# New places for tail rows, the second piece of T1 and tiles of x, and another last tile in a four-layer graph network

## The chip, the cores and the metric

The kernel runs on one core of one Trainium2 chip. The metric is the device time of one execution in microseconds (us), where a smaller number is better. Three timed runs of the kernel before gave 2122.76, 2124.17 and 2127.33 us, so the median is 2124.17 us.

The core has a matrix engine (TensorE, "PE" in the profile, with its weight loads shown as "PEld"), three engines for other arithmetic (VectorE "DVE", ScalarE "ACT", GpSimd "POOL") and SyncE "SP". Each works through its own list of instructions in order and waits on semaphores. SP and POOL also issue the transfers between the memory outside the core (DRAM) and the core's buffer (SBUF). The sums of matrix products arrive in PSUM, of which this kernel uses five banks under the tag `agg`, two under `out` and one under `sm`.

## The reference

There are N = 2708 nodes with 512 features. Each of four layers normalizes x by row, applies relu, multiplies by the adjacency matrix and by a weight, and adds the result to x:

```python
h = relu(layernorm(x)); x = x + relu((dinv[:, None] * (adj + I) * dinv[None, :]) @ h @ W0)
h = relu(layernorm(x)); x = x + (dis[:, None] * adj * dis[None, :]) @ h @ W1.T + b1
h = relu(layernorm(x)); x = x + relu((dinv[:, None] * (adj + I) * dinv[None, :]) @ h @ W2)
h = relu(layernorm(x))
# layer 3: attention over the edges (x_a) and a plain aggregation (x_b), each with a gate
x = x + sigmoid(attn_a * (softmax_like(scores, adj != 0) @ (h @ W_sa)) + attn_b * (adj @ (h @ W_g) + b_g))
```

Here `dinv` and `dis` are reciprocal roots of the row sums of adj, with 1 and with 1e-8 added.

## The kernel before, in words

**Tiling.** The 2708 rows are cut into four quarters of 677. A quarter holds five full tiles of 128 rows (`KT = 5`, 20 full tiles in all) and 37 tail rows. The tails of all quarters share two more tiles: tile `NF = 20` has 32 rows from each quarter, and tile `NF + 1` has the last 5 rows of each, padded to 8. The columns of a quarter are handled in two pieces of `W = 339`, numbered u = 0 and 1. A block of the transposed adjacency matrix is a 128 x 5 x 339 array in fp32, 848 KB.

**The aggregation** computes the transpose of adj @ h into `agg`. The 20 full tiles go through a product scheme with 7 in place of 8 multiplications, on two levels. The outer level forms sums of blocks named y11, y21, y22, t1, t2, t3 and t4. For each of these and each u, `inner_x` and `inner_y` form the sums of the inner level (DVE, lines 447 to 485), and `multiply` (line 515) runs seven products of ten matmuls each into banks pa, pb, pc and pd. `give` hands the results on to `agg`. `inner_y` takes four blocks o11, o12, o21 and o22. It writes t1, t2 and t4 to a pool of three buffers and t3 to a place that it is given, or into o12 where it is given none.

**The first aggregation** (`first_aggregate`, line 662) also builds the t sums and stores them in DRAM (`keep_o`, line 418, on POOL's queue), because later layers load them. Its last part is what the change touches:

1. u = 0 of the product with t4 is made. The four blocks of t2 become those of t1 by taking away y22, one block at a time (`third_less`, the subtraction at line 828). The blocks of y22 pass through two buffers, `y22[0]` and `y22[1]`.
2. `tails(True, (0, 1), rows)` adds the products of the tail rows for quarters 0 and 1 (lines 571 and 576, `agg` additions at line 621). `tail_rows` loads the rows of a quarter and adds a piece of the identity to them (line 600, DVE). Those of quarter 0 are loaded early. Those of quarter 1 go to a block from `free`, which at that point is `y22[0]`. They are two transfers of 339 KB, in runs of 2712 bytes.
3. The four blocks of T1 for u = 1 are loaded (`accumulated`: a load by SP, then a transfer by POOL that adds another block, line 712). Their places are `t4[3]`, `more[2]`, `y22[1]` and `y22[0]`.
4. Product 5 (with T1) runs for u = 0 and 1. For u = 0 its t3 goes to the place `own_t3`. A sum over half of h, `XC += XA` (line 868), stands between the two.
5. `tails(True, (2, 3), rows)` follows, then the epilogue of the first half of the tiles, product 3 with XC, and the epilogue of the rest.

**The epilogues** of layers 0 to 2 (`next_x`, line 893) go through tiles in groups of three. `load_x` brings a tile of x to one of four places of 512 columns (`xt_places`, taken in turn, POOL's queue, line 890). PE multiplies by the weight (line 883), ACT applies relu and the scale (line 903) into one of two places `y`, DVE adds it to x (line 908) and takes statistics, POOL stores x (line 909), and after the group ACT writes the normalized tiles to h (line 223). All these places, like `misc` (four times 512 columns) and `bg_bc` (512 columns, for a bias of layer 3), are slices of one tile `ends`. `misc` holds the bias of layer 1 in its first quarter and, from layer 2 on, four vectors of scores (`score_vectors`). The two vectors for quarters 2 and 3 of `misc` are loaded at line 968, and the bias at line 1044.

**Layer 3's last stage** (line 1163) runs 40 steps over the quarters, and each tile of the output is finished by `attention` (line 1111): load x and the gated sum, one short matmul for the row sum, a projection by `W_sa` (512 columns, 8 matmul instructions), three operations on DVE and ACT, and the store. Five tiles are left after the last step: 17, 18 and 19, then tail tiles 20 and 21. A tail tile first collects its columns with copies on DVE (`tile_cols`, lines 174 and 160) into the two places `y`, and leaves through four stores, one for each quarter.

**Order.** A scheduler fixes the order of each engine's instructions when the program is compiled. It takes what it holds to be ready first, with earlier lines first among the ready. `tc.issue_after(ins)` puts the instructions of a block behind `ins` on the same engine's list.

Of the kernel before, what the change touches and what calls it, by code (L numbers as in the profile page):

```python
# [8 lines left out]
FP = mybir.dt.float32  # L9
AF = mybir.ActivationFunctionType  # L10
ALU = mybir.AluOpType

P = 128
D = 512
NC = D // P
# [6 lines left out]
U = 2  # L22
W = (Q + 1) // U
NF = NQ * KT
# [13 lines left out]
def gnn_kernel(  # L38
# [20 lines left out]
    nc = tc.nc  # L59
# [10 lines left out]
    ps_out = ctx.enter_context(tc.tile_pool(name="ps_out", bufs=2, space=bass.MemoryType.PSUM))  # L70
# [40 lines left out]
    agg = big.tile([P, 2, 2, 2, 2, U * W], FP, name="agg")  # L111
# [12 lines left out]
    free = list(in_obuf)  # L124
    more = [block(ends, k * BLK) for k in range(3)]
    own_t3 = block(ends, 3 * BLK)
# [5 lines left out]
    misc, ends_o = ends[:, ends_o : ends_o + 4 * D], ends_o + 4 * D  # L132
    xt_places = [ends[:, ends_o + k * D : ends_o + (k + 1) * D] for k in range(GT + 1)]
# [3 lines left out]
    bg_bc = ends[:, ends_o : ends_o + D]  # L137
# [10 lines left out]
    def load_w(w):  # L148
        w_sb = w_place[:, 0 : NC * D].rearrange("p (c o) -> p c o", c=NC)
        nc.gpsimd.dma_start(w_sb, w.rearrange("(c p) o -> p c o", p=P))  # L150
        return w_sb

    def full_cols(a, t):
        k = t % KT
        return a[:, k * P : (k + 1) * P]
# [7 lines left out]
    def tile_cols(a, t):  # L163

        cs = [a[:, f, :, c] for f in range(a.shape[1]) for c in range(a.shape[3])]
        if t < NF:
            q = t // KT
            return [full_cols(c[:, q // 2, q % 2], t) for c in cs]
        o, m = (KT * P, R0) if t == NF else (KT * P + R0 - PAD, R1P)
        if a.shape[5] == R0 + R1:  # L170
            o -= KT * P
        g = new_y().rearrange("p (c n) -> p c n", c=NC)
        for c, src in enumerate(cs):
            nc.vector.tensor_copy(
                g[:, c, 0 : NQ * m].rearrange("p (i q r) -> p i q r", i=2, q=2),
                src[:, :, :, o : o + m],
            )
        repeat(g[:, 0 : len(cs)], NQ * m)
        return [g[:, c] for c in range(len(cs))]
# [133 lines left out]
    y11 = {}  # L313
# [78 lines left out]
    XA = h[:, 0:half, 0 : D // 2]  # L392
    XB = h[:, 0:half, D // 2 : D]
    XC = h[:, half:NF, 0 : D // 2]
# [12 lines left out]
    QUAD = [(0, 0), (0, 1), (1, 0), (1, 1)]  # L407
# [36 lines left out]
    at_v, at_u2, at_u3, at_end, at_shift, at_y, at_pe = [], [], [], [], [], [], []  # L444
# [26 lines left out]
    def inner_y(blks, u, loops, t3=None, t3_first=False):  # L471
        o11, o12, o21, o22 = blks
        if loops:
            add_loops(o11, u, loops)
            add_loops(o22, u, loops)
        t1, t2, t4 = (tpool.tile([P, KT, W], FP, tag="t", name=f"t{k}") for k in (1, 2, 4))
        t3 = o12 if t3 is None else t3
        if t3_first:
            nc.vector.tensor_add(t3, o22, o12)
        nc.vector.tensor_add(t1, o12, o11)  # L480
        nc.vector.tensor_add(t2, o22, t1)  # L481
        at_y.append(nc.vector.tensor_add(t4, o21, t2).ins)  # L482
        if not t3_first:
            at_y[-1] = nc.vector.tensor_add(t3, o22, o12).ins
        return {1: o11, 2: o21, 3: o22, 4: t4, 5: t1, 6: t2, 7: t3}
# [94 lines left out]
    def tail_rows(self_loops, q, pieces=None):  # L580


        blk = None
        if pieces is None:
            blk = free.pop(0)
            both = blk[:, 0 : 2 * U].rearrange("p (s u) w -> p s u w", s=2)
            pieces = [both[:, :, u] for u in range(U)]
            for s in range(2):
                nc.sync.dma_start(both[:, s], yt[s, :, q])
        else:  # L590
            for u in range(U):
                load_tails(q, u, pieces[u])
        if self_loops:
            o = (KT * P) % W
            for s, i, c0, n in (
                (0, ident[:, q * R0 : (q + 1) * R0], o, R0),
                (1, again_ident[:, q * R1P + PAD : (q + 1) * R1P], o + R0, R1),
            ):
                d = pieces[U - 1][:, s, c0 : c0 + n]
                nc.vector.tensor_add(d, d, i)  # L600
        return blk, pieces
# [60 lines left out]
    def first_aggregate(epilogue):  # L662
# [9 lines left out]
        pieces = [(q, u) for q in range(2) for u in range(U)]  # L672
        t3 = {0: early[:2]}
        places = spare + early[2:]
        for q, u in pieces:
# [14 lines left out]
            if (q, u) == (1, 0):  # L690
                ys = inner_y([y11[a, b, u] for a, b in QUAD], u, 0, own_t3, True)
# [12 lines left out]
        def accumulated(blks, key, u, source):  # L704

            for (a, b), blk in blks.items():
                if key in PLAIN:
                    load_plain(key, a, b, u, blk)
                else:
                    nc.sync.dma_start(blk, osum[key, a, b, u])  # L710
                j, i = PLAIN[source]
                last = nc.gpsimd.dma_start(blk, yb[j + a, i + b, u], accum_op=ALU.add)
            return last.ins

        def keep_all(blks, key, u, a_b=QUAD):
            for a, b in a_b:
                keep_o(blks[QUAD.index((a, b))], key, a, b, u)
# [8 lines left out]
        came = {}  # L726
# [116 lines left out]
                    )  # L843
        for k, y in ((0, y22[0]), (1, y22[1]), (2, y22[0]), (3, y22[1])):
            minus_y22 = third_less(k, y, at_y[-1])
        free += y22
        with tc.issue_after(at_end[-1]):
            rows = [early_rows, tail_rows(True, 1)]
        tails(True, (0, 1), rows)
        t1 = [t2u, [t4[3], more[2], free.pop(0), free.pop(0)]]  # L850
        assert not free
        came = accumulated({QUAD[k]: t1[1][k] for k in (0, 1, 3, 2)}, "y12", 1, "y11")
        with tc.issue_after(at_end[-1]):
            nc.vector.tensor_add(agg[:, 1, 0], agg[:, 1, 0], agg[:, 1, 1])
        xs_ = inner_x(XB)
        p5 = [(0, 1, "less"), (1, 1, "less")]
        for u in range(U):
            more_loops = OUTER[5][2] - (OUTER[6][2] if u == 0 else 0)
            if u == 1:
                with tc.issue_after(came):  # L860
                    keep_all(t1[u], "t1", u, QUAD[1:3])
            with tc.issue_after(minus_y22 if u == 0 else at_end[-3]):
                ys = inner_y(t1[u], u, more_loops, own_t3 if u == 0 else None)
            keep_all(t1[u], "t1", u, QUAD if u == 0 else QUAD[::3])
            multiply(xs_, ys, u, p5)
            if u == 0:
                with tc.issue_after(at_end[-1]):
                    nc.vector.tensor_add(XC, XC, XA)
        free += t2u + [f for f in t1[1] if f is not more[2]]
        with tc.issue_after(at_end[-3]):  # L870
            rows = [tail_rows(True, q) for q in (2, 3)]
# [7 lines left out]
    def project(w_sb, t):  # L879
        cs = tile_cols(agg, t)  # L880
        po = ps_out.tile([P, D], FP, tag="out", name="po")
        for c in range(NC):
            nc.tensor.matmul(  # L883
                po, cs[c], w_sb[:, c, :], start=(c == 0), stop=(c == NC - 1)
            )
        return po, cs
# [32 lines left out]
                    after(t)  # L919


    w_sb = []

    def first_epilogue(ts):
# [60 lines left out]
    def keep_h(t):  # L985
        nc.gpsimd.dma_start(hs[t], h[:, t, :])
        h_dots(behind.get(t, ()))

    w2_sb = load_w(w2)
    vs = None  # L990

# [47 lines left out]
    def again(ts, fs):  # L1039

        for t in ts:
            nc.sync.dma_start(h[:, t, fs], hs[t][:, fs])

    nc.gpsimd.dma_start(bg_bc, bg.partition_broadcast(P))
    parts = {1: range(12, 14), 7: range(14, 17), 2: range(17, 20), 4: range(20, NT)}
    hooks = {p: lambda ts=ts: h_dots(ts) for p, ts in parts.items()}
# [55 lines left out]
    def place(t):  # L1102

        if t < NF:
            o = (t // KT) * Q + (t % KT) * P
            return [(0, P, o)]
        if t == NF:
            return [(q * R0, R0, q * Q + KT * P) for q in range(NQ)]
        return [(q * R1P + PAD, R1, q * Q + KT * P + R0) for q in range(NQ)]

    def attention(t, columns):
        xt = load_x(t, xs)
        y = load_x(t, xbs)
        nc.scalar.activation(xt, xt, AF.Copy, bias=0.5)
        sm = ps_sm.tile([P, NT], FP, tag="sm", name="pse")
        nc.tensor.matmul(sm[:, 0:1], columns(t), ones[:, 0:1], start=True, stop=True)
        pE, _ = project(wsa_sb, t)
        g = small.tile([P, 1], FP, tag="ge", name="ge")
        nc.vector.tensor_add(g, sm[:, 0:1], eps[:, t : t + 1])
        nc.vector.reciprocal(g, g)  # L1120
        nc.vector.tensor_mul(g, g, ga[:, t, 0:1])
        nc.vector.scalar_tensor_tensor(y, pE, g, y, ALU.mult, ALU.add)
        nc.scalar.activation(y, y, AF.Tanh, scale=0.5)
        nc.vector.scalar_tensor_tensor(xt, y, 0.5, xt, ALU.mult, ALU.add)
        for o, n, to in place(t):
            nc.gpsimd.dma_start(out[to : to + n, :], xt[o : o + n, :])

    sums = misc[:, 0 : 2 * U * W + NQ * (R0 + R1)]
    tail_sums = sums[:, 2 * U * W :].rearrange("p (f i c q r) -> p f i c q r", f=1, i=2, c=1, q=2)
# [32 lines left out]
    todo = []  # L1162
    for n, (q, u, b) in enumerate(steps):
# [35 lines left out]
        elif todo:  # L1199
            t, se_t = todo.pop(0)  # L1200
            attention(t, lambda t, se_t=se_t: full_cols(se_t, t))
    for t, se_t in todo:
        attention(t, lambda t, se_t=se_t: full_cols(se_t, t))
    for t in (NF, NF + 1):
        attention(t, lambda t: tile_cols(tail_sums, t)[0])


# [59 lines left out]
```

## Time and profile before

| What | Value |
|---|---|
| Timed runs, median | 2124.17 us |
| Profiled execution, its own time | 2125.74 us |
| Its span, first to last instruction | 2123.7 us |
| DVE busy | 1412.9 us |
| ACT busy | 406.0 us |
| POOL busy | 182.3 us |
| DMA, mean rate over the span | 170 GB/s |
| Mean granted clock of PE | 0.994 |

The profile describes one execution. Its span leaves out 2.0 us of the execution's own time, and the execution is 1.6 us above the median of the timed runs. A line of the timeline gives the start, the duration, the engine, the source line, the operation, what it writes and reads with the shapes, and in brackets the idle time of the engine just before it with what ended that idle time. A line of the waits gives the waiting instruction, what it waited for, the total in us, the number of times and the longest. "L600" is line 600 of the kernel.

### The profile page before, as it was taken

The page shows a single profiled execution, that of the slowest core. Times are in us where ns is not written, and L with a number is a line of the kernel's source. Part 1 is how long each engine was busy: PE and PEld are TensorE (multiplying, and loading weights), DVE is VectorE, ACT ScalarE, POOL GpSimd, SP SyncE. Part 2 cuts the span into 40 slices and gives each one's busy share as a digit, 9 for nine tenths or more (in the row PEclk, how much of TensorE's full clock was granted, in tenths as well). Part 3 has the DMA queues.
Part 4 walks back from the last instruction along what each step waited for, and adds up shares of the span by engine and source line. Part 5 has one row for each costly group of instructions (what it writes and reads, how often), then busy time and mean ns, then how long its engine had stood idle before and what let it go on. Part 6 is the DMA issues. An engine that isn't in the chain of part 4 may idle for free.

```text
span 2123.7 us, 20033 instructions
## 1 busy us (share of the span) xinstructions
PE 2064.4 (97%) x7320; PEld 1286.0 (61%) x7320; DVE 1412.9 (67%) x2486; ACT 406.0 (19%) x826; POOL 182.3 (9%) x329
## 2 busy tenths in 40 slices
PE   5999989999999999999999999999999999999998
PEld 2666645546666554666664556666777666666664
DVE  4578866656777767866685789867538755566512
ACT  1430001130000011100002120000117533444401
POOL 0110111120000011100002130000001000000001
PEclk9999999999999999999999999999999999999999
DMA  9998593545545444655444565545451223232212
GB/s 368 299 373 269 186 337 124 193 172 182 178 157 177 138 171 139 229 176 173 164 143 165 198 219 175 181 164 177 154 174 74 92 89 117 87 108 90 84 37 65
DMA packets 79442, 360.86 MB, mean 170 GB/s; under 512 B 10620, under 2 KB 15100, under 8 KB 79216
## 3 DMA queue, kind: packets, MB, share of 16 engines
q1 hardware_dynamic: 50384, 245.43, 33.8%
q0 software_dynamic: 28960, 114.15, 16.6%
q8 instruction: 58, 0.95, 0.2%
q14 instruction: 40, 0.33, 0.0%
HBM read 294.61 MB, written 62.15 MB: 168 GB/s over the span
## 4 chain that ended last, share of the span: by engine, by line
issue 45%; PE 39%; DMA 7%; DVE 5%; POOL 3%; ACT 0%; POOLq 0%; SPq 0%; DVEq 0%; ACTq 0%
PE pa L509 9%; PE pc L509 9%; PE pd L509 9%; PE pb L509 5%; PE po L883 3%; DMA obuf<-in_yb_dram 2%; PE pt L571 2%; DMA ends<-xs 2%; PE pg L1022 1%; DMA obuf<-in_yt_dram 1%; POOL ends L890 1%; POOL xs L909 1%; DVE ends L908 1%; PE pt L576 1%; DVE ends L975 1%
## 5 line engine op out<-in xcount | busy, mean ns | idle before, releaser
L1174 PE MATMUL pe<-obuf,h 128*128 128x339 f32 x1280 | 372.8, 448 | 0.0
L509 PE MATMUL pa<-obuf,h 128*128 128x339 f32 x1040 | 316.4, 448 | 2.9 <-ACT v L543 1.5
L1174 PEld LDWEIGHTS pe<-obuf,h 128*128 128x128 f32 x1280 | 240.9, 189 | 126.6 <-issue 10.0
L883 PE MATMUL po<-ends,agg 128*128 128x512 f32 x640 | 281.7, 596 | 4.6 <-ACT ends L903 4.3
L509 PEld LDWEIGHTS pa<-obuf,h 128*128 128x128 f32 x1040 | 196.1, 189 | 107.9 <-issue 6.9
L883 PEld LDWEIGHTS po<-ends,agg 128*128 128x128 f32 x640 | 119.6, 190 | 147.8 <-issue 137.5
L1095 ACT ACTIVATE e<-r,nsr 128x339 f32<-128x339 f32 x352 | 170.7, 566 | 27.4 <-DVE obuf L1099 11.6
L509 PE MATMUL pb<-t,s 128*128 128x339 f32 x560 | 171.1, 452 | 2.6 <-DVE t L481 2.6
L509 PE MATMUL pc<-t,h 128*128 128x339 f32 x560 | 169.4, 448 | 2.7 <-DVE u L556 2.7
L509 PE MATMUL pd<-t,s 128*128 128x339 f32 x560 | 169.2, 448 | 0.0
L509 PE MATMUL pd<-obuf,s 128*128 128x339 f32 x550 | 166.5, 448 | 1.9 <-DVE agg L530 1.9
L543 ACT COPY v<-pa 128x339 f32<-128x339 f32 x56 | 24.6, 440 | 733.7 <-PE pa L509 730.7
L509 PEld LDWEIGHTS pb<-t,s 128*128 128x128 f32 x560 | 106.3, 191 | 57.9 <-DVE t L481 4.0
L509 PEld LDWEIGHTS pc<-t,h 128*128 128x128 f32 x560 | 105.8, 189 | 57.7 <-DVE u L556 3.8
L509 PEld LDWEIGHTS pd<-t,s 128*128 128x128 f32 x560 | 105.9, 189 | 54.4 <-issue 0.5
L509 PEld LDWEIGHTS pd<-obuf,s 128*128 128x128 f32 x550 | 104.0, 189 | 55.8 <-DVE agg L530 3.4
L509 PE MATMUL pc<-obuf,s 128*128 128x339 f32 x440 | 133.1, 448 | 0.0
L509 PEld LDWEIGHTS pc<-obuf,s 128*128 128x128 f32 x440 | 83.3, 189 | 42.8 <-issue 0.5
L481 DVE TENSOR_TENSOR t<-obuf,t 128x1695 f32<-128x1695 f32 x55 | 105.4, 1916 | 0.0
L909 POOL DMA_DIRECT2D xs<-ends x66 | 35.9, 544 | 797.4 <-DVE ends L908 713.6
L482 DVE TENSOR_TENSOR t<-obuf,t 128x1695 f32<-128x1695 f32 x52 | 99.6, 1916 | 0.1
L1191 DVE COPY agg<-pe 128x339 f32<-128x339 f32 x16 | 7.5, 506 | 138.1 <-PE pe L576 138.1
(262 smaller groups left out, 2300.3 us busy)
## 6 DMA issues: line engine op xcount, KB each, us to landing
obuf<-in_yb_dram SPq DMA_DIRECT2D x132, 847.5 KB, 4.5
obuf<-osumt SPq DMA_DIRECT2D x100, 847.5 KB, 4.4
osumt<-obuf POOLq DMA_DIRECT2D x22, 847.5 KB, 11.0
xs<-ends POOLq DMA_DIRECT2D x66, 256.0 KB, 2.3
ends<-xs POOLq DMA_DIRECT2D x66, 256.0 KB, 3.5
obuf<-in_yt_dram SPq DMA_DIRECT2D x30, 339.0 KB, 3.6
obuf<-in_yb_dram POOLq DMA_DIRECT2D x11, 847.5 KB, 10.2
ends<-in_yb_dram SPq DMA_DIRECT2D x9, 847.5 KB, 9.2
```

Source lines behind the costliest of these rows:

```text
L481: nc.vector.tensor_add(t2, o22, t1)
L482: at_y.append(nc.vector.tensor_add(t4, o21, t2).ins)
L509: last = nc.tensor.matmul(ps, x[:, k, :], y[:, k, :], start=start and k == 0, stop=k == KT - 1, skip_group_check=not start,)
L543: at_v.append(nc.scalar.copy(v, pa).ins)
L571: nc.tensor.matmul(ps[c], h[:, NF, c * P : (c + 1) * P], tl[:, 0, :], start=start, stop=False)
L576: nc.tensor.matmul(ps[c], h[g, NF + 1, c * P : (c + 1) * P], tl[g, 1, :], start=False, stop=True)
L883: nc.tensor.matmul(po, cs[c], w_sb[:, c, :], start=(c == 0), stop=(c == NC - 1))
L890: nc.gpsimd.dma_start(xt, src[t])
L908: nc.vector.tensor_add(xt, xt, y)
L909: nc.gpsimd.dma_start(xs[t], xt)
L1095: nc.scalar.activation(e[:, k], row, AF.Exp, bias=nsr[:, t, s : s + 1], scale=1.0)
L1174: nc.tensor.matmul(pe[c], h[:, t, c * P : (c + 1) * P], a, start=(t == 0), stop=False)
```

## The change

It has four groups of edits.

- **Tail rows of quarter 1** go to the first four slices of `own_t3`, as two pieces with two transfers each (four of 173 KB, in runs of 1356 bytes). They, with the identity additions, are queued behind the last subtraction of y22 and no longer behind the last `give` of t4.
- **T1.** The blocks for u = 1 get the places `y22[0]`, `more[2]`, `y22[1]` and `t4[3]`, loaded in the order 1, 0, 2, 3. For u = 0, t3 is formed in o12 itself, and o12 and o21 are stored before `inner_y`. `XC += XA` moves behind the sums of u = 1.
- **Places for x.** Layers 0 and 1 get seven (quarters 2 and 3 of `misc`, and `bg_bc`, are added), layer 2 five (`bg_bc`), layer 3 four until its last step. The loads of lines 968 and 1044 then wait until those uses are over.
- **The end.** The five last tiles get twelve places in four blocks of `obuf`. The order becomes 17, 21, 18, 20, 19, and tile 19 is projected, finished and stored by halves of 256 columns.

```diff
-        free += y22
-        with tc.issue_after(at_end[-1]):
-            rows = [early_rows, tail_rows(True, 1)]
+        own = own_t3[:, 0 : 2 * U].rearrange("p (s u) w -> p s u w", s=2)
+        with tc.issue_after(minus_y22):
+            rows = [early_rows, tail_rows(True, 1, [own[:, :, u] for u in range(U)])]
         tails(True, (0, 1), rows)
-        t1 = [t2u, [t4[3], more[2], free.pop(0), free.pop(0)]]
+        t1 = [t2u, [y22[0], more[2], y22[1], t4[3]]]
         assert not free
-        came = accumulated({QUAD[k]: t1[1][k] for k in (0, 1, 3, 2)}, "y12", 1, "y11")
+        came = accumulated({QUAD[k]: t1[1][k] for k in (1, 0, 2, 3)}, "y12", 1, "y11")
...
-            if u == 1:
-                with tc.issue_after(came):
-                    keep_all(t1[u], "t1", u, QUAD[1:3])
+            with tc.issue_after(came) if u == 1 else nullcontext():
+                keep_all(t1[u], "t1", u, QUAD[1:3])
             with tc.issue_after(minus_y22 if u == 0 else at_end[-3]):
-                ys = inner_y(t1[u], u, more_loops, own_t3 if u == 0 else None)
-            keep_all(t1[u], "t1", u, QUAD if u == 0 else QUAD[::3])
+                ys = inner_y(t1[u], u, more_loops)
+            keep_all(t1[u], "t1", u, QUAD[::3])
             multiply(xs_, ys, u, p5)
-            if u == 0:
-                with tc.issue_after(at_end[-1]):
-                    nc.vector.tensor_add(XC, XC, XA)
+        with tc.issue_after(at_y[-1]):
+            nc.vector.tensor_add(XC, XC, XA)
...
+    misc_places = [misc[:, k * D : (k + 1) * D] for k in (2, 3)]
+    xt_places += misc_places + [bg_bc]
...
+    xt_places = [p for p in xt_places if not any(p is m for m in misc_places)]
     w2_sb = load_w(w2)
...
+    xt_places = [p for p in xt_places if p is not bg_bc]
     nc.gpsimd.dma_start(bg_bc, bg.partition_broadcast(P))
...
-    def attention(t, columns):
+    def attention(t, columns, pieces=1):
...
-        pE, _ = project(wsa_sb, t)
+        cs = tile_cols(agg, t)
...
-        nc.vector.scalar_tensor_tensor(y, pE, g, y, ALU.mult, ALU.add)
-        nc.scalar.activation(y, y, AF.Tanh, scale=0.5)
-        nc.vector.scalar_tensor_tensor(xt, y, 0.5, xt, ALU.mult, ALU.add)
-        for o, n, to in place(t):
-            nc.gpsimd.dma_start(out[to : to + n, :], xt[o : o + n, :])
+        n = D // pieces
+        for k in range(pieces):
+            f = slice(k * n, (k + 1) * n)
+            pE = ps_out.tile([P, n], FP, tag="out", name="pE")
+            for c in range(NC):
+                nc.tensor.matmul(pE, cs[c], wsa_sb[:, c, f], start=(c == 0), stop=(c == NC - 1))
+            nc.vector.scalar_tensor_tensor(y[:, f], pE, g, y[:, f], ALU.mult, ALU.add)
+            nc.scalar.activation(y[:, f], y[:, f], AF.Tanh, scale=0.5)
+            nc.vector.scalar_tensor_tensor(xt[:, f], y[:, f], 0.5, xt[:, f], ALU.mult, ALU.add)
+            for o, m, to in place(t):
+                nc.gpsimd.dma_start(out[to : to + m, f], xt[o : o + m, f])
...
-    for t, se_t in todo:
-        attention(t, lambda t, se_t=se_t: full_cols(se_t, t))
-    for t in (NF, NF + 1):
-        attention(t, lambda t: tile_cols(tail_sums, t)[0])
+    flat = [blk.rearrange("p k w -> p (k w)") for blk in free[:4]]
+    xt_places = [a[:, k * D : (k + 1) * D] for a in flat for k in range(3)]
+    todo = [(t, lambda t, se_t=se_t: full_cols(se_t, t)) for t, se_t in todo]
+    for k, t in ((1, NF + 1), (3, NF)):
+        todo.insert(k, (t, lambda t: tile_cols(tail_sums, t)[0]))
+    for n, (t, columns) in enumerate(todo):
+        attention(t, columns, 1 if n + 1 < len(todo) else 2)
```

## The prediction

> **What bounds the kernel now.** I read the page's busy times first, then everything PE waited for, then the timeline around the two places that the diff touches.
>
> ```profile
> PE 2064.4 (97%) x7320; PEld 1286.0 (61%) x7320; DVE 1412.9 (67%) x2486; ACT 406.0 (19%) x826; POOL 182.3 (9%) x329
> ```
>
> PE is the bound. No edit takes a matmul away, so a gain can only come from PE's idle time, from a slow clock after it, or from what follows PE's last matmul. PE's waits, longest first:
>
> ```profile
> PE pt L571 <- DVE agg L621: 7.4, 2, 6.6
> PE po L883 <- ACT ends L903: 4.3, 3, 2.0
> PE pc L509 <- DVE u L556: 2.7, 2, 2.0
> PE pb L509 <- DVE t L481: 2.6, 2, 2.2
> PE pd L509 <- DVE agg L530: 1.9, 1, 1.9
> PE pc L509 <- DVE ends L484: 1.8, 1, 1.8
> PE po L883 <- DVE ends L160: 1.8, 1, 1.8
> ```
>
> The 6.6 us wait is the largest after the start of the program. In the timeline, DVE's list shows its cause:
>
> ```profile
> 272.54 0.19 DVE L600 TENSOR_TENSOR obuf<-obuf,ident 128x32 f32<-128x32 f32 x1 [1.32 <-DMA obuf<-in_yt_dram]
> 275.54 0.17 DVE L600 TENSOR_TENSOR obuf<-obuf,again_ident 128x5 f32<-128x5 f32 x1 [2.80 <-DMA obuf<-in_yt_dram]
> ...
> 278.19 1.75 DVE L621 TENSOR_TENSOR agg<-agg,pt 128x339 f32<-128x339 f32 x4
> ...
> 278.74 2.63 PE L571 MATMUL pt<-tl,h 128*128 128x339 f32 x4 [6.63 <-DVE agg L621]
> ```
>
> L600 waits for quarter 1's tail rows; two sums (L468, L480) and then the L621 that frees PE's bank stand behind it. After the idle time PE also runs slowly (columns: time, PE busy, clock, DMA share, GB/s):
>
> ```profile
> 278.74:284.73 5.99, 5.99 (x16) 0.50 1.05 383
> ```
>
> Half a clock for 6.0 us costs 3.0 us of PE's work. DMA is full at the same time, its packets split evenly between POOL's queue q0 and SP's q1 from 264 to 276 us:
>
> ```profile
> q0 software_dynamic: 437, 2.60, 70.8%
> q1 hardware_dynamic: 408, 1.40, 31.8%
> ```
>
> The end, from the timeline:
>
> ```profile
> 2110.54 5.40 PE L883 MATMUL po<-ends 128*128 128x512 f32 x8 [1.82 <-DVE ends L160]
> ...
> 2115.97 0.75 DVE L1122 SCALAR_TENSOR_TENSOR ends<-po,ge,ends 128x512 f32<-128x512 f32 x1 [3.03 <-PE po L883]
> ...
> 2118.40 2.01 POOL L1126 DMA_DIRECT2D out_dram<-ends  x4 [3.17 <-DVE ends L1124]
> ```
>
> The last projection starts 1.82 us late and takes 5.40 us where the four before it take 3.68.
>
> **What the Trainium skill says.** "TensorE: Matmul & The Clock Gate", Part 1: a monitor with a free-running window of 3.4 us halves PE's clock after idling and restores it after a busy window. The trace agrees, at 284.73 and again at the end, where 1.82 us of idling was enough. The same page, on the engine queues: ACT and DVE are strictly first in, first out; the trace shows L468 held behind L600. "DMA: Bandwidth & Descriptors", Queues, rings and completion order: an engine takes descriptors of one ring in order and alternates between rings by packet; 437 against 408 packets agree.
>
> **The end.** Twelve places let the ten loads of the five tiles be issued while the last step runs, so no x or xbs load is late (before, L1114 waited 4.36, 2.83 and 2.87 us). Tail tiles 21 and 20 come second and fourth, so their copies (four of L174 at 0.17 to 0.26 us, two of L160 at 0.23 and 0.29) run beside a full tile's 3.66 us of PE; the place y they need is free one tile earlier. PE then runs five projections without a gap: 2093.93 + 5 x 3.66 = 2112.2 instead of 2115.95 (halves cost nothing: 257-column matmuls at L1022 ran at 25.53 / 117 = 0.218 us, half of 512 columns' 0.43). For the last half, DVE, ACT and DVE take an estimated 0.40, 0.37 and 0.36 us by size (from 0.75, 0.63, 0.69) and 0.4 of gaps: 1.5 instead of 2.45. One store issue takes 0.55 instead of 2.01; the four of tile 20 leave POOL at about 2113.1, before it. The 3.3 us after the last issue stay. End: 2112.2 + 1.5 + 0.55 + 3.3 = 2117.6, **-6.1 us**; bounds -7 and -3 (if one copy chain still stalls PE and slows the clock).
>
> **T1, second piece.** For u = 1 PE idles 0.53 (L543), 2.23 (L481) and 1.84 us (L484), 4.6 in all. The late block was the one in `y22[0]`: its load was issued at 290.44, after PE had read the tail rows there, and the added block landed at 312.18. Now it can be loaded from 263.94, when the third subtraction ends; even behind everything on SP's ring I put the last added block before 300, 10 us ahead of need. `XC += XA` (2.82 us) leaves the list before L482 and L484. DVE's list then has L480 and L481 ready 4.0 us after product 5's first piece ends and L484 at 8.6, where PE wants them at 4.1 and 9.3: only about 0.7 is left, **-3.9**; bounds -4.6 and 0. The moved sum lies behind L484 beside some 9 us of PE work. The in-place t3 waits for the store of o12, issued at 260.39 and landed at 274.19, before L484's 281.69; uncovered, each us late is paid. The two stores moved ahead are the ones that POOL issued first anyway.
>
> **Tail rows of quarter 1.** They can be issued from 258.7 (PE done with `own_t3`), 5 us earlier. But SP's ring already holds y22's last block until about 265, and POOL's ring holds an adding block (packets of 525 ns until 269.5) and the stores of T1. With runs of 1356 instead of 2712 bytes the rows are 512 packets instead of 256, and alternation gives them one for each of q0's. Estimate: 8 per DMA engine beside the adding block (8 x 0.585 = 4.7 us), 16 beside the two stores (16 x 0.305 = 4.9), 8 alone (0.5): 265 + 10.1 = 275.1, and with the lag of 1 to 2 us seen before about 276.5, against 275.5 now. The wait stays. L600 may also now stand before the loop additions L431 (six, 1.1 us) and the last give L530 (0.4), which then follow the wait. L621 comes 1 to 3 us later, PE's slow stretch overlaps more of its idle time: **+1.3**. Bounds: -5.5 (rows there at 270; the sums still hold PE about 2 us) and +9 (all 512 packets at the adding pace, 32 x 0.585 = 18.7 us).
>
> **Places for x.** L908's waits are:
>
> ```profile
>   DMA ends<-xs: 37.5, 10
>   DMA ends<-in_x_dram: 17.9, 5
> ```
>
> Most is covered. PE paid 1.38 us in layer 0 (379.85) and 0.99 + 0.71 + 1.96 + 1.02 + 1.92 = 6.6 in layer 2. Seven places cover two groups, so the 1.4 goes. Five in layer 2 let two of three loads go ahead; the third waits as now but is wanted 3.4 us later than the second, and the load waits of 5 to 7 us shrink below the cover of two banks and two places y. DVE is also full there with h_dots (L975), so I take 2.6 of 6.6: **-4.0**; bounds 0 and -8. Loads of lines 968 and 1044 leave POOL's list at 325 and 290 and run where nothing waits for them soon: 0.
>
> **Sum.** -6.1 - 3.9 + 1.3 - 4.0 = -12.7. The profiled execution took 2125.74 us (2123.7 of span), giving 2113.0; from the median 2124.17 it is **2111.5**.
>
> **Rivals.**
> - *Rows in time.* Rows land by 271 and the tails gain 4.5: 2124.2 - 6.1 - 3.9 - 4.5 - 4.0 = 2105.7. For it: the earlier issue. Against: the full rings.
> - *Rows slower.* DVE sits before L600 until about 283, +8, with x giving 1.4 only: 2124.2 - 6.1 - 3.9 - 1.4 + 8 = 2120.8. For it: the doubled packets.
> - *Hidden anyway.* T1 and x free nothing because DVE's own list holds PE: 2124.2 - 6.1 + 1.3 = 2119.4. For it: DVE had no pause at most of those waits.
> - *Slower: o12's store queued late.* If POOL's list puts it behind all three adding transfers, the last of which cannot start before about 289, it lands at 302; L484 then blocks 12 of the L621, and PE waits from 283. 19 - 14 = +5: 2129. It decides only from a landing at about 301 on. Against it: that store was issued long before those transfers.
>
> **How the numbers follow.** As worked (2108 to 2116): 0.55. Rows in time: 0.14. Rows slower: 0.12. Hidden anyway: 0.11. Slower: 0.05, other new orders 0.03. 0.2% is 4.2 us, about what a measurement of this kernel can tell from no change. Faster: the first two, 0.09 of hidden and 0.05 of slower rows, 0.83; same: 0.10; slower: 0.07. 2105 to 2119.5 holds the likeliest case, most of the first and third rivals and part of the second: about 0.8.
>
> **What would show it.** No PE gap between the five last projections, clock 1.00 there, one store issue at the end. Rows landing at 275 to 278 and a PE gap of 6 to 9 us before L571. No gap at L481 and L484 in T1's second piece, the last added block landed before 300. Layer 0's gap at L883 gone, layer 2's about halved. Wrong: rows near 270, a store of o12 after 290, or new gaps in POOL-fed epilogues.

## The result and the profile after

The kernel after takes 2111.43 us (median of six runs, 2108.52 to 2113.16) against 2125.63 us for the kernel before on the same chip (six runs). The ratio is 0.9933, with a 95% interval of 0.992 to 0.9945, so the change gained 14.2 us. The forecast was 2111.5 us, a gain of 12.7 us. The profiled execution took 2109.49 us with a span of 2107.3 us.

PE's busy time, from the page of the kernel after:

```profile
PE 2059.4 (98%) x7328; PEld 1284.3 (61%) x7328; DVE 1414.6 (67%) x2488; ACT 406.8 (19%) x827; POOL 182.8 (9%) x330
```

PE is still the bound. The eight extra matmuls are the last tile's halves. What PE waited for from 60 us on, kernel after, longest first:

```profile
PE pt L571 <- DVE agg L530: 7.8, 1, 7.8
PE pc L509 <- DVE u L556: 2.6, 4, 1.2
PE pt L571 <- DVE agg L621: 2.1, 2, 1.6
...
```

The waits of the weight product for ACT (4.3 us in the kernel before), those for L481 and L484 in T1's second piece, and the 1.82 us at the last tile are gone or below 1 us. One wait has grown: quarter 1's tail rows. The timeline of the kernel after shows it (DVE's lines, then PE's):

```profile
275.19 0.19 DVE L600 TENSOR_TENSOR ends<-ends,ident 128x32 f32<-128x32 f32 x1 [6.98 <-DMA ends<-in_yt_dram]
275.87 0.17 DVE L600 TENSOR_TENSOR ends<-ends,again_ident 128x5 f32<-128x5 f32 x1 [0.48 <-DMA ends<-in_yt_dram]
275.95 1.05 DVE L431 SCALAR_TENSOR_TENSOR obuf<-ident,obuf 128x128 f32<-128x128 f32 x5
276.91 0.51 DVE L530 TENSOR_TENSOR agg<-pd,u 128x339 f32<-128x339 f32 x1
...
277.47 1.50 PE L571 MATMUL pt<-tl,h 128*128 128x339 f32 x2 [7.77 <-DVE agg L530]
280.61 2.63 PE L571 MATMUL pt<-tl,h 128*128 128x339 f32 x4 [1.64 <-DVE agg L621]
```

L600 now stands ahead of five L431 and of the last L530, as the prediction said that it may. PE therefore waits twice: first for the L530, then for the L621 behind L468 and L480. After the gaps PE runs slowly for a while. By the window of the tails behind the second gap, kernel after (columns as before):

```profile
280.61:291.68 11.07, 11.07 (x45) 0.77 1.06 255
```

DMA is full during the wait (its share is 1.03 from 269.70 to 277.47 us). SP's queue moved 1.49 MB in 710 packets from 264 to 276 us, where the kernel before moved 1.40 MB in 408.

The end, from the timeline of the kernel after:

```profile
2097.95 3.70 PE L1130 MATMUL pE<-ends,agg 128*128 128x256 f32 x16
...
2103.38 0.54 POOL L1135 DMA_DIRECT2D out_dram<-obuf  x1 [0.38 <-DVE obuf L1133]
```

The last projection takes 3.70 us at the full clock, with no gap before it, and one store issue follows. The wait of the addition to x (L908 before, L906 after) on loads of layers 0 to 2, kernel after:

```profile
  DMA ends<-xs: 6.4, 3
```

This was 37.5 us in ten waits before, and the 17.9 us on `in_x_dram` have no line any more.

**Where the time went, by stage.** I cut the span at PE instructions that every kernel has. "Tails and T1" runs from the first L571 of the first aggregation to the first weight product of layer 0. Each layer runs from its first weight product to the next aggregation's first L571; "end" runs from the first gate product to the end of the span. All in us, from the profiled execution of each kernel:

| Stage | before | after | end alone | places alone | rows and T1 alone | layer 0 only |
|---|---|---|---|---|---|---|
| tails and T1 | 81.3 | 79.8 | 80.1 | 80.3 | 80.5 | 79.8 |
| layer 0 | 277.4 | 276.0 | 277.7 | 276.0 | 277.7 | 276.0 |
| layer 1 | 281.7 | 280.2 | 281.7 | 280.1 | 283.5 | 283.7 |
| layer 2 | 283.9 | 279.6 | 283.4 | 280.5 | 284.4 | 284.1 |
| end | 612.1 | 606.3 | 606.6 | 612.1 | 611.1 | 606.6 |

The first stage splits where product 5 begins. The tails before it went from 22.87 to 25.96 us (+3.1), and what follows from 58.45 to 53.86 us (-4.6). The first L571 itself comes 1.65 us earlier after (265.7 against 267.4 us), in code that the change leaves alone; in the other runs of kernels with the same code up to there it comes between 266.6 and 268.6 us. I don't count that as the change's.

The same code does not take the same time in every execution. "Tails and T1" is unchanged in the kernels "end alone" and "places alone", yet took 80.1 and 80.3 us there: the tails 22.24 and 22.47 us, what follows 57.84 and 57.85. The end is unchanged in "rows and T1 alone" and took 1.0 us less; its last projection did not run slowly there. In layer 1, "rows and T1 alone" and "layer 0 only" each contain one slow stretch of 3.41 us, which is 1.7 us of PE's work; the kernel before has none there.

### The profile page after: what moved, and what is told of

Same layout as the page of the kernel before. It is cut to its first block, busy times and chain, and to the rows that moved or that the text cites. A ratio compares the mean times of both kernels' runs of the same rounds, so it can differ in the third digit from the quotient of the medians.

```text
span 2107.3 us, 20074 instructions
## 1 busy us (share of the span) xinstructions
PE 2059.4 (98%) x7328; PEld 1284.3 (61%) x7328; DVE 1414.6 (67%) x2488; ACT 406.8 (19%) x827; POOL 182.8 (9%) x330
## 4 chain that ended last, share of the span: by engine, by line
PE 86%; DVE 6%; DMA 4%; issue 2%; POOL 1%; ACT 0%; SPq 0%; POOLq 0%; DVEq 0%; ACTq 0%
PE pe L1183 17%; PE pa L509 14%; PE pc L509 13%; PE pd L509 13%; PE po L881 9%; PE pb L509 7%; PE pE L1130 4%; PE pg L1024 3%; PE pt L571 3%; DMA obuf<-in_yb_dram 2%; PE pt L576 1%; PE pe L571 1%; DMA ends<-in_yt_dram 1%; DMA ends<-xs 1%; DVE ends L976 1%
## 5 line engine op out<-in xcount | busy, mean ns | idle before, releaser
L509 PE MATMUL pa<-obuf,h 128*128 128x339 f32 x1040 | 315.8, 448 | 2.5 <-ACT h L223 1.4
L509 PEld LDWEIGHTS pa<-obuf,h 128*128 128x128 f32 x1040 | 196.1, 189 | 106.3 <-issue 5.5
L881 PE MATMUL po<-ends,agg 128*128 128x512 f32 x480 | 207.6, 593 | 0.0
L509 PE MATMUL pc<-t,h 128*128 128x339 f32 x560 | 169.7, 449 | 2.7 <-DVE u L556 2.6
L509 PE MATMUL pb<-t,s 128*128 128x339 f32 x560 | 171.1, 452 | 1.1 <-DVE s L441 0.7
L509 PE MATMUL pd<-t,s 128*128 128x339 f32 x560 | 169.0, 448 | 0.0
L509 PE MATMUL pd<-obuf,s 128*128 128x339 f32 x550 | 166.3, 448 | 0.3 <-DVE agg L530 0.3
L543 ACT COPY v<-pa 128x339 f32<-128x339 f32 x56 | 24.7, 440 | 722.5 <-PE pa L509 719.4
L881 PEld LDWEIGHTS po<-ends,agg 128*128 128x128 f32 x480 | 90.9, 190 | 114.3 <-issue 109.3
L509 PEld LDWEIGHTS pc<-t,h 128*128 128x128 f32 x560 | 105.5, 189 | 58.7 <-DVE u L556 5.4
L509 PEld LDWEIGHTS pb<-t,s 128*128 128x128 f32 x560 | 106.4, 191 | 56.7 <-issue 1.8
L509 PEld LDWEIGHTS pd<-t,s 128*128 128x128 f32 x560 | 105.9, 189 | 54.1
L509 PEld LDWEIGHTS pd<-obuf,s 128*128 128x128 f32 x550 | 104.1, 189 | 53.8 <-DVE agg L530 1.3
L509 PE MATMUL pc<-obuf,s 128*128 128x339 f32 x450 | 136.1, 448 | 0.0
L509 PEld LDWEIGHTS pc<-obuf,s 128*128 128x128 f32 x450 | 85.1, 189 | 43.8 <-issue 0.5
L481 DVE TENSOR_TENSOR t<-obuf,t 128x1695 f32<-128x1695 f32 x55 | 105.5, 1918 | 0.0
## 6 DMA issues: line engine op xcount, KB each, us to landing
obuf<-in_yb_dram POOLq DMA_DIRECT2D x11, 847.5 KB, 11.7
```

The costliest lines, as they stand in the source:

```text
L509: last = nc.tensor.matmul(ps, x[:, k, :], y[:, k, :], start=start and k == 0, stop=k == KT - 1, skip_group_check=not start,)
L543: at_v.append(nc.scalar.copy(v, pa).ins)
L881: nc.tensor.matmul(po, cs[c], w_sb[:, c, :], start=(c == 0), stop=(c == NC - 1))
```

## Experiments

All ratios are to the kernel before on the same chip. The kernel before had a median of 2125.63 us beside the kernel after, and of 2124.55 to 2124.98 us beside the experiments. So a difference "by the medians" between an experiment and the kernel after is uncertain by about 1 us from this alone.

**The parts one by one.** Each kernel is the kernel before with one part of the change: only the end; only the places for x; only the rows and T1.

```diff
 # end alone: attention in pieces, twelve places, the new order
+    xt_places = [a[:, k * D : (k + 1) * D] for a in flat for k in range(3)]
+    for k, t in ((1, NF + 1), (3, NF)):
+        todo.insert(k, (t, lambda t: tile_cols(tail_sums, t)[0]))
...
 # places alone: misc's quarters 2 and 3 and bg_bc
+    xt_places += misc_places + [bg_bc]
...
 # rows and T1 alone
-            rows = [early_rows, tail_rows(True, 1)]
+            rows = [early_rows, tail_rows(True, 1, [own[:, :, u] for u in range(U)])]
-        t1 = [t2u, [t4[3], more[2], free.pop(0), free.pop(0)]]
+        t1 = [t2u, [y22[0], more[2], y22[1], t4[3]]]
```

> The kernel before with the edits of the end alone (twelve places, order 17, 21, 18, 20, 19, the last tile by halves). If the parts of the change act independently, this takes 5.8 us off, as the stage of the end does in the two traces: median near 2119.8, PE without a gap between its five last projections, clock 1.00 there and one store issue last. If the end only looks shorter because the whole program reached it at a better moment of the clock's window, it takes off 4 us or less (the 1.8 us gap stays away, the slow window does not).

> The kernel before with the places for x alone (seven, seven, five). Theory: PE's waits in the epilogues came from late loads of x; then 1.4 us goes in layer 0, about 1.5 in layer 1 and about 4.3 in layer 2, 7.2 in all, median near 2118.4, and DVE's waits on loads of x at its addition fall from 55 us to under 10. Rival: only layer 0's gap came from loads, the rest of the 7.2 us came from the new order that follows from the earlier parts of the change; then 1.4 to 2 us, median near 2124.

> The kernel before with the edits of the tail rows and of T1 alone. Theory: the tails cost 3.1 us more and T1's second piece 4.6 us less, so a net of -1.5 us, median near 2124.1, which is below what the timing tells; in its trace the gap before L571 is 7 to 9 us (6.6 before) and the gaps at L481 and L484 are gone. Rival: T1's gain comes with the places for x (an emptier POOL list and DMA), then the gaps at L481 or L484 are there and the net is +1 to +3 us.

| Kernel | Median us | Ratio | 95% interval |
|---|---|---|---|
| end alone | 2119.82 | 0.9981 | 0.9973 to 0.9988 |
| places alone | 2116.77 | 0.9965 | 0.9954 to 0.9976 |
| rows and T1 alone | 2124.34 | 1.0001 | 0.9993 to 1.0009 |

By these ratios the parts are worth 4.0, 7.4 and -0.2 us of 2125 us, 11.2 in sum; the whole is worth 14.2, with an interval from 11.7 to 17, so the sum does not contradict it. The stage table is finer. The end alone takes 5.5 us off its stage (612.1 to 606.6); some 1.0 of this is the slow last projection, which one kernel with the old end did not have either. The places alone take off 1.4, 1.6 and 3.4 us in layers 0, 1 and 2. Rows and T1 lose 3.8 us before product 5 (26.68 against 22.87) and gain 4.6 behind it (53.85 against 58.45): two effects of opposite sign, which a time alone would have called nothing. The stages of the other experiments agree with these sizes: the eight further kernels with the places took 275.9 to 276.1 us in layer 0, 279.6 to 280.9 in layer 1 and 278.3 to 280.5 in layer 2.

**What holds PE before product 5.** First, quarter 1's tails multiplied after product 5's first piece, so that its rows have some 20 us more:

```diff
-        tails(True, (0, 1), rows)
+        tails(True, (0,), [early_rows])
...
             multiply(xs_, ys, u, p5)
+            if u == 0:
+                after_u0 = at_end[-3]
+                with tc.issue_after(after_u0):
+                    row = tail_rows(True, 1, [own[:, :, v] for v in range(U)])
+                tails(True, (1,), [row])
```

> The changed kernel, with quarter 1's tail rows multiplied after product 5's first piece in place of before it. If L600 waiting for the rows at the head of DVE's list is the whole cause of the gaps of 7.8 and 1.6 us and of the slow clock after them (3.3 us of PE's work), some 2.3 us of gap stay (PE ahead of DVE's sums for a bank), and 8 to 10 us go: median near 2102.5, clock 1.00 from 270 to 290 or one slow window. If PE would have to wait there anyway, because DVE's sums for T1 or the blocks are late, the gap moves to L509 and less than 3 us go: above 2108.

It took 2109.52 us (0.9928, 0.9915 to 0.994), which the intervals don't tell apart from the kernel after, and not the 8 to 10 us less that were expected. In the stage of tails and T1 it is 2.7 us (77.1 against 79.8). The timeline of this run shows where the rest went (PE, then DVE, then PE):

```profile
274.59 2.40 PE L571 MATMUL pt<-tl,h 128*128 128x339 f32 x4 [2.15 <-DVE agg L621]
...
300.87 0.61 DVE L431 SCALAR_TENSOR_TENSOR obuf<-ident,obuf 128x45 f32<-128x45 f32 x3 [2.90 <-DMA obuf<-in_yb_dram]
...
306.88 2.63 PE L571 MATMUL pt<-ends,h 128*128 128x339 f32 x4 [2.25 <-DVE agg L621]
```

The 7.77 us are gone, so the rows had caused them. But the tails wait again at their new place, 1.34 us and then the 2.25 us of the last line, and PE was slow for 6.83 us from 305.57 us on. By the trace the cause is another late transfer: L431 stands 2.90 us at the head of DVE's list for a block of T1, and the sums of the second piece and L621 stand behind it. In the kernel after this L431 comes at 310.52 us and waits for nothing. So with the tails out of the way product 5 begins earlier (278.34 us against 291.68), and its second piece comes before its last block. The rival was right in this, though the gap stands at the tails and not at L509. The next place to try is after product 5, where quarters 2 and 3 go through together anyway:

```diff
-        own = own_t3[:, 0 : 2 * U].rearrange("p (s u) w -> p s u w", s=2)
-        with tc.issue_after(minus_y22):
-            rows = [early_rows, tail_rows(True, 1, [own[:, :, u] for u in range(U)])]
-        tails(True, (0, 1), rows)
+        tails(True, (0,), [early_rows])
...
-            rows = [tail_rows(True, q) for q in (2, 3)]
-        tails(True, (2, 3), rows)
+            rows = [tail_rows(True, q) for q in (1, 2, 3)]
+        tails(True, (1, 2, 3), rows)
```

> Before product 5 only quarter 0's tail rows are multiplied; quarters 1, 2 and 3 follow together after it, and quarter 1's rows take a free block as those of 2 and 3 do. Theory (the rows' landing at 275.84 us, then the last give, hold PE for 7.77 + 1.64 us, with 13.65 us of slow clock after it): both gaps shrink to one of about 2.2 us and at most one or two slow windows of 3.4 us remain, some 8 us less than the changed kernel: about 2102. Rival (PE waits for DVE's list and not for the rows): the gap stays at 6 us or more or comes back at another place, within 3 us of the changed kernel.

It took 2101.05 us (0.989, 0.9874 to 0.9905): 10.4 us less than the kernel after by the medians, of which 8.0 us lie in the stage of tails and T1 (71.8 against 79.8). PE's gaps there:

```profile
274.62 1.41 PE L571 MATMUL pt<-tl,h 128*128 128x339 f32 x4 [2.15 <-DVE agg L621]
...
302.99 3.12 PE L509 MATMUL pb<-t,s 128*128 128x339 f32 x10 [1.76 <-DVE t L481]
```

The clock stayed at 1.00 all through. The first gap, of 2.15 us, is left by the order of DVE's list: L468 and L480 stand ahead of L621. The second, of 1.76 us, is T1's last block again: L431 waits 2.05 us for it until 298.24 us. The next kernel is this one with the sums of u = 0 queued behind the second L621 of quarter 0's tails:

```diff
+        second_add = at_end[-7]
...
-            with tc.issue_after(minus_y22 if u == 0 else at_end[-3]):
+            with tc.issue_after(second_add if u == 0 else at_end[-3]):
```

> As the run with quarter 1's tails last, and the sums for u = 0 (L480 and L481 before product 5) are queued behind the second addition L621 of quarter 0's tails. Theory: what then holds PE before product 5 is DVE's order of the sums ahead of L621, so the gap of about 2.2 us goes and the kernel gains another 1 to 3 us: 2099 to 2101. Rival: the sums come late for product 5's first matmul instead and the time stays within 1 us of the other run.

It took 2100.04 us (0.9883, 0.9869 to 0.9898). PE's timeline:

```profile
279.07 3.12 PE L509 MATMUL pb<-t,s 128*128 128x339 f32 x10 [1.55 <-DVE t L481]
286.05 3.13 PE L509 MATMUL pc<-obuf,s 128*128 128x339 f32 x10 [1.00 <-DVE obuf L484]
```

The tails no longer wait, but product 5 now waits for its sums, 1.55 and 1.00 us: part of the gain comes back as the rival said. The stage still shrinks by 1.9 us (69.9 against 71.8), but in the run before it the 1.76 us gap at T1's late block is part of it, and here that block came in time. Without that gap the two stages would be 0.2 us apart. The medians differ by 1.0 us, which the intervals don't tell apart, so a gain by this edit is not shown. This kernel has the lowest median of the study, 1.2% faster than the kernel before and 0.5% faster than the kernel after.

**Why the rows are late.** The kernel after, with the same place and time of issue, but two transfers in runs of 2712 bytes:

```diff
+        elif whole is not None:
+            for s in range(2):
+                nc.sync.dma_start(whole[:, s], yt[s, :, q])
...
-            rows = [early_rows, tail_rows(True, 1, [own[:, :, u] for u in range(U)])]
+            rows = [early_rows, tail_rows(True, 1, [own[:, :, u] for u in range(U)], own)]
```

> The changed kernel, with quarter 1's rows loaded to the same place as two transfers in runs of 2712 bytes (256 packets) and not four in runs of 1356 (512 packets). Theory (SP's and POOL's queues alternate packet by packet, so shorter runs get a smaller share of the bytes): the rows land about 3 us earlier, near 272.5 us, and the gap before L571 is about 5 us and not 7.77; 2 to 5 us less than the changed kernel. Rival (their place behind y22's last block and the queue's bytes decide): landing and gap within 0.7 us of the changed kernel's.

It took 2108.03 us (0.9921, 0.9905 to 0.9938), 3.4 us less than the kernel after by the medians, though the intervals overlap; its stage of tails and T1 is 3.2 us shorter (76.6 against 79.8). DVE's and PE's timeline (line 603 is the L600 of the kernel after):

```profile
273.37 0.17 DVE L603 TENSOR_TENSOR ends<-ends,again_ident 128x5 f32<-128x5 f32 x1 [3.04 <-DMA ends<-in_yt_dram]
...
274.97 1.50 PE L571 MATMUL pt<-tl,h 128*128 128x339 f32 x2 [4.33 <-DVE agg L530]
```

The rows landed 6.70 us after the first L571, against 10.13 us in the kernel after, and the gap shrank from 7.77 to 4.33 us. The bytes, the place and the queue are the same; the number of packets is halved. Scatter does not explain this: in the six executions with the short runs the second L600 began 9.6 to 10.9 us after the first L571, here 6.72. The queues show the mechanism, in 7 us in which both had work. From 266 to 273 us, kernel after:

```profile
q0 software_dynamic: 335, 2.05, 84.0%
q1 hardware_dynamic: 335, 0.41, 17.1%
```

From 265 to 272 us, this run:

```profile
q0 software_dynamic: 253, 1.53, 76.0%
q1 hardware_dynamic: 261, 0.66, 25.0%
```

The queues send one packet each in turn, so with short packets SP's moves 0.41 MB where it moved 0.66. The short packets are not slow in themselves: by these shares of 16 engines I estimate 0.06 us for one, against 0.11 for a long one. This agrees with the Trainium skill, "DMA: Bandwidth & Descriptors", Queues, rings and completion order: a DMA engine goes round its rings packet by packet. That a queue with shorter packets then gets fewer bytes follows from it and is what the run shows.

The tails before product 5 take 22.77 us, where the kernel before took 22.87. With long runs the rows did land earlier than in the kernel before (6.7 against 8.2 us after the first L571), but L600 ahead of the last L530 takes as much back, as the next run shows. Long runs together with the old order were not run.

**L600 ahead of the last give.** The kernel after, with DVE's part of the rows queued behind the last `give`, as before:

```diff
-        with tc.issue_after(minus_y22):
+        with tc.issue_after(at_end[-1]):
```

> The changed kernel, with DVE's part of quarter 1's rows (L600) queued behind the last give as in the kernel before, so that five L431 and the last L530 (1.56 us) come ahead of the wait. Theory (of the 3.1 us that the edit on the rows costs, about 1.6 come from this order): the two gaps of 7.77 + 1.64 us become one that ends about 1.6 us earlier, 1 to 2 us less than the changed kernel, about 2110. Rival (the landing alone decides): no change beyond 0.5 us.

It took 2111.74 us (0.9939, 0.9924 to 0.9954), no less than the kernel after. PE has the one large gap that was expected:

```profile
281.00 2.63 PE L571 MATMUL pt<-tl,h 128*128 128x339 f32 x4 [7.83 <-DVE agg L621]
```

In this execution the rows landed at 277.76 us, 10.84 us after the first L571 and not 10.13. From the landing to product 5 it took 14.19 us, against 15.84: 1.65 us shorter, the length of five L431 and one L530 (1.56). So the order costs what it should, once the landing is given. In the total this doesn't show, and with over 1 us of scatter in the landing alone I can't say from these runs that the edit gains anything.

**XC += XA.** The kernel after, with the sum back between the two pieces of product 5:

```diff
-        with tc.issue_after(at_y[-1]):
-            nc.vector.tensor_add(XC, XC, XA)
+            if u == 0:
+                with tc.issue_after(at_end[-1]):
+                    nc.vector.tensor_add(XC, XC, XA)
```

> The changed kernel with the sum XC += XA (2.82 us) back between the two pieces of product 5. Theory (the gap of 1.84 us before L484's matmul in the kernel before was this sum standing ahead of L484 on DVE): that gap comes back at 1.5 to 2 us, the one before L481 (2.23 us) does not, since the block behind that one now lands early. Rival (both gaps were the late block): no gap comes back. In time 1 to 3 us more, or none.

It took 2112.66 us (0.9943, 0.9928 to 0.9957), and in the stage of tails and T1 2.0 us more (81.8 against 79.8). From its timeline:

```profile
318.32 2.82 DVE L867 TENSOR_TENSOR h<-h 128x2560 f32<-128x2560 f32 x1
...
322.89 1.92 DVE L484 TENSOR_TENSOR ends<-obuf,ends 128x1695 f32<-128x1695 f32 x1
...
324.86 3.13 PE L509 MATMUL pc<-ends,s 128*128 128x339 f32 x10 [1.72 <-DVE ends L484]
```

The gap before L484's matmul is back (1.84 us in the kernel before), and the one before L481's (2.23 us) is not. So T1 had two separate waits, and XC's place made the second. For the first, DVE's timeline of the kernel before shows the late block:

```profile
312.20 0.61 DVE L431 SCALAR_TENSOR_TENSOR obuf<-ident,obuf 128x45 f32<-128x45 f32 x3 [2.52 <-DMA obuf<-in_yb_dram]
```

L480 and L481 stand behind it, and in the kernel after L431 does not wait. No run changed the blocks' places alone.

**Places in layers 1 and 2.** The kernel after, with seven places in layer 0 and four from layer 1 on:

```diff
+    xt_places = [p for p in xt_places if not any(p is m for m in misc_places + [bg_bc])]
     w1_sb = load_w(w1)
```

> The changed kernel with the seven places for x in layer 0 alone: layers 1 and 2 have four, as before. Theory (places gained 1.4 us in layer 0, 1.5 in layer 1, 4.3 in layer 2): PE's gaps before the weight product in layers 1 and 2 come back, 5 to 6 us more than the changed kernel: about 2117. Rival (layer 1's and 2's part of the difference is chance of the clock windows, and the prediction's 2.6 is the share of the places): 2.5 to 3 us more: about 2114.

It took 2118.13 us (0.9967, 0.9954 to 0.998): 6.7 us more than the kernel after. Layer 1 lost 3.5 us and layer 2 4.5 (the table's last column). PE's waits of this run from 730 to 1400 us, from 1.5 us up (in the kernel after none of them is longer than 1.2 us at a time):

```profile
PE pc L509 <- DVE u L556: 3.5, 2, 2.4
PE po L881 <- ACT ends L901: 3.0, 2, 1.8
PE pd L509 <- DVE agg L530: 1.7, 1, 1.7
PE po L881 <- DVE ends L174: 1.5, 2, 1.0
```

Two of the four rows of this run are not at the weight product at all: L556 and L530 belong to the aggregation's products, which go on between the groups of tiles. In layer 1 the gap is 2.37 us before L509, waiting for L556, and the clock was at 0.50 for the 3.41 us from 864.48 on. That slow stretch is 1.7 of the 3.5 us, and the kernels before and "end alone", with gaps of 1.99 and 1.96 us there, did not have it. So for this part the rival, chance of the clock's windows, holds. Layer 2 has no slow stretch in either run.

**Halves.** The kernel after, with the last tile whole:

```diff
-        attention(t, columns, 1 if n + 1 < len(todo) else 2)
+        attention(t, columns)
```

> The changed kernel with the last tile whole, not by halves. Theory (DVE, ACT, DVE on 512 columns take 0.75, 0.63 and 0.69 us, on 256 columns 0.48, 0.42 and 0.42): from PE's last matmul to the last store's issue 2.5 us instead of 1.7, about 0.8 us more in all. Rival (the second half's operations and its second row of matmuls cost as much as they hide): within 0.3 us of the changed kernel at that stage.

It took 2112.83 us (0.994, 0.9924 to 0.9957). From PE's last matmul to the last store's issue it takes 2.5 us instead of 1.7, and to the end of the span 6.6 instead of 5.6. The halves are worth 0.9 us of the end's 5.8.

## Why the prediction was right, step by step

The time was right to 0.1 us, but that is luck. The terms were off in both directions, and the base was low: the forecast starts from the 2124.17 us of three runs, and six runs gave 2125.63 us. From there its -12.7 us would have given 2112.9. The forecast of the gain was 1.5 us short.

| Term | Predicted | Measured by stage |
|---|---|---|
| the end | -6.1 | -5.8 |
| T1, second piece | -3.9 | -4.6 |
| tail rows of quarter 1 | +1.3 | +3.1 |
| places for x | -4.0 | -7.2 |
| sum | -12.7 | -14.5 |

- **The end** was right in its mechanism and its size. PE's last matmul ends 3.7 us earlier, counted from the first gate product; what follows it takes 5.6 us instead of 7.7.
- **T1** was right in both causes, by the XC run and the wait at 312.20 us. Of its 4.6 us, 0.6 is within what the same code varies by. The last added block landed at 296.49 us, where the prediction put it before 300. The 0.53 us (L543) is left, where it allowed 0.7 us. The store of o12 landed at 272.53 us, so the rival "slower" was nowhere near its 301 us.
- **Tail rows.** The landing (275.84 us, predicted 275 to 278) and the gap (7.77 us, predicted 6 to 9) were right, and so was the reason, twice as many packets: the run with long runs shows it. The size was short. The order was foreseen as something that may happen and was not added in full: it costs 1.65 us from the landing on. A second gap of 1.64 us comes with it, and the slow clock lasted 13.65 us instead of 10.24. The mis-sized term is "L621 comes 1 to 3 us later ... +1.3": counted from the first L571, L621 came 3.5 us later (14.34 against 10.83), and the slow stretch did not overlap more idle time alone but cost PE 3.3 us instead of 3.0 (an estimate from PE's busy time and clock in its windows). The tails took 3.1 us longer in the kernel after, and 3.8 in the run of this part alone.
- **Places for x.** Layer 0's 1.4 us were right to the tenth. Two terms were mis-sized. "2.6 of 6.6" in layer 2 was too little: five places gave 4.3 us, and 4.5 went when they were taken away. And layer 1 was not in the sum at all, though it gained 1.5 us. The prediction had looked for gaps at the weight product (L883). Layer 1's largest gap stood at another line, L509 for L556, 14 us after the last wait for x (L908 at 849.36 us, 1.88 us). The kernel before, DVE's and PE's timeline:

```profile
860.70 0.61 DVE L431 SCALAR_TENSOR_TENSOR obuf<-ident,obuf 128x45 f32<-128x45 f32 x3 [2.84 <-DMA obuf<-in_yb_dram]
...
865.80 3.13 PE L509 MATMUL pc<-t,h 128*128 128x339 f32 x10 [1.99 <-DVE u L556]
```

The wait for x is not what this gap comes from: at 851.28 us DVE stood idle again, for PE. After that it waited 2.84 us for a block of the matrix and 0.87 us, until 862.18, for a vector that the scores need; L556 stands behind both. The block's load was issued at 852.42 us, when PE had ended ten matmuls that its list splits around the last weight product. The vector's load stands on POOL's list behind the store of the tile of x from that weight product. In the kernel after the ten matmuls come ahead of the last weight product, the block's load was issued at 842.75 us, L431 waited 1.40 us, and PE's gap was 0.95 us. So with more places the scheduler chose another order in layer 1, which the sum had put at nothing there. How much comes from this order and how much from the waits for x stays open; no run separates them.

Of the rivals, "rows in time" and "rows slower" did not occur, and "hidden anyway" fell with the XC run and with the places alone.

## What to carry to other kernels

When a transfer is moved to an earlier time, count its packets as well as its bytes: cutting the same rows into runs half as long made them land 3.4 us later here, and that was more than the earlier issue brought. A gap need not come from the nearest wait that one knows of: in layer 1 two other loads stood between the wait for x and the gap, so follow the chain back from the gap to the wait that ended last, and look at other lines than the edited one, since an edit can change the scheduler's order there. And when late work is moved away, what follows comes earlier and can find its own data missing: with quarter 1's tails between the two pieces of product 5 a block of T1 was 2.90 us late, and the stage gained 2.7 us; beside the other tails it gained 8.0.

## What was unexpected in the hardware

The Trainium skill, in "TensorE: Matmul & The Clock Gate", Part 1, gives a full idle window of about 3.4 us as what slows the clock. Gaps well below that did here: 1.82 us at the end of the kernel before, 2.37 us in layer 1 of the run with the places in layer 0 alone. But the length alone does not decide. The run with quarter 1's tails between the pieces and the run with them last have the same gap of 2.15 us, ending at 274.59 and at 274.62 us. By windows, the first ran at 0.50 right after it, and the second did not (its own windows line):

```profile
274.86:278.27 3.41, 3.41 (x12) 0.50 1.01 419
```

```profile
274.62:277.90 3.28, 3.28 (x16) 1.00 1.01 424
```

This agrees with the page's free-running window, whose position differs from one execution to the next. Slow stretches lasted 3.41, 6.83, 10.24 or 13.65 us, multiples of 3.41, so I take their ends as the window's edges. In the first run an edge lies at 274.86 us, and the whole gap falls into the window before it. In the second a slow stretch ended at 130.24 us; 42 windows of 3.413 us later, by my estimate, an edge lies at 273.60 us and cuts the gap into 1.13 and 1.02 us. So here a gap of about 2 us cost either nothing more or another 1.7 us, by whether it fell into one window. The limit isn't sharp in these traces: by the same estimate T1's gap of 1.84 us in the kernel before (322.36 to 324.20 us) also lay in one window and slowed nothing.
